# A graph-attention layer on one core: copies of the group loop moved to ScalarE, other superblock sizes at the end, the last quad divided by groups

## The chip, the cores and the metric

The kernel runs on one core of one Trainium2 chip. The metric is the device time of one execution in microseconds (us), less is better. Engines are called TensorE (PE in profiles), VectorE (DVE), ScalarE (ACT), GpSimd (POOL) and SyncE (SP).

## What is computed

A graph with 12,500 nodes of 128 features and 200,000 edges, sorted by destination. Each node's features are normalised and clipped at zero, multiplied by a weight matrix, and each edge gets four attention logits (one per head). Per destination node the logits go through a softmax over the incoming edges, and the source rows are summed with those weights.

```
h   = (max(layernorm(x), 0) @ W_node.T).reshape(N, 4, 32)
att = leaky(a . [h[src], h[dst], (edge_attr @ W_edge.T).reshape(E, 4, 32)])
m   = max(segment_max(att, dst), 0)
ex  = exp(att - m[dst])
denom = segment_sum(ex, dst) + (E - degree) * exp(-m)
out = x + segment_sum(ex / denom[dst] * h[src], dst)
```

## The kernel before

**Tiling.** Edges lie in 392 groups of 511 (four columns of 128 lanes, `J` = 4). Lane 0 of column 0 is kept for a row that carries the partial sum of a node from the group before. Four groups are a quad (98 of them, `QG` = 4), and a few quads a superblock. A group's destinations lie in a window of 96 nodes (`WIN`). A node's table row (`ROW` = 137 numbers) holds four heads of 32 values with a one behind each, a count of one (`R_CNT`) and four source logits (`R_SRC`).

**Stages.** A node stage writes the table. GpSimd meanwhile gathers raw node rows for quads 0 to 3, which `converted` (L236) later turns into table rows on the core: transposes, a copy, matmuls, copies by ScalarE (L262), then two memsets of ones by VectorE (L264, L266). From quad 4 on, `gather` (L127) fetches table rows: one indirect DMA per group and column (L136), 16 per quad, into a `ga` buffer of which there are 8. The buffer comes free when the sums of the quad eight places earlier are done.

**The group loop** has four kinds of steps per quad or superblock:

- `fetch` (L471): edge features `ea`, destinations `db`, side rows `pw`, node rows `xw`, issued by SyncE two quads ahead; `db` has two buffers.
- `logits` (L492) for each group: one comparison by VectorE (L499), six matmuls (L504, L507); then `add_sources` (L510) per quad, two VectorE instructions, of which L521 is the first to read the gathered rows.
- `softmax` (L532) per superblock: a chain of about twenty VectorE instructions on tiles of 511 columns, with transposes by TensorE and two exps by ScalarE (L589, L591).
- `sums` (L642) per quad: two small VectorE copies (L653 into `hot`, L654 from the PSUM tile `ex_ps` into `ga`); then for each group L660 (rows times weights), L663 (one-hot of the destinations), three matmuls (L668), and `complete` (L616), which works one group late: for the group before, L633 scales the carried row out of the PSUM tile `acc`, L637 copies its count, and the last matmul L639 follows; for the group before that, L624 copies `acc` to `pt`. One group after a quad's last copy, `divide` (L673) makes the output of all four groups with six VectorE instructions (L679 to L692) and SyncE writes four windows (L695). Windows of neighbouring groups overlap.

**Order.** The order on each engine is the order written here; nothing reorders it. `together` takes one step of each generator in turn. For superblock s the main loop (L769) runs `sums` of the last quad of s-1 beside the logits of the first quad of s+1 and the softmax of s; then `sums` of each quad of s but the last, each beside the logits of one more quad of s+1; logits left over follow alone. `add_sources` of a quad comes at the next logits or softmax, so L521 of a superblock's last quad stands at the start of its softmax. The end (L786 to L789) is `sums` of quad 97 and three calls of `complete`.

Superblocks are sized by `ends` (L427): two of 2 quads in front, then 22 of 4, then 2, 2, 1, 1.

Of the kernel before, what the change touches and what calls it, by code (L numbers as in the profile page):

```python
# [12 lines left out]
OP = mybir.AluOpType  # L13
AX = mybir.AxisListType

P = 128
H, HD = 4, 32
HW = HD + 1
D = H * HD
# [3 lines left out]
TINY = 1e-30  # L23


R_CNT, R_SRC, ROW = H * HW, H * HW + 1, H * HW + 5

J = 4
GE = J * P
NE = GE - 1  # L30
WIN = 96
QG = 4
# [3 lines left out]
NODE_T = 9  # L36
RAW = 4
SETS = max(NODE_T, QG * J)
PAD = 1 << 20


def blocks(total, step):
    return [(i, min(step, total - i)) for i in range(0, total, step)]
# [3 lines left out]
def kernel(  # L47
# [35 lines left out]
    nc = tc.nc  # L83
# [21 lines left out]
    ones = consts.tile([P, P], F32, name="ones")  # L105
# [7 lines left out]
    is_last = consts.tile([P, G, J], BF16, name="is_last")  # L113
# [5 lines left out]
    quads = blocks(G, QG)  # L119
    nq = len(quads)  # L120
# [26 lines left out]
    with tc.manual_schedule():  # L147
# [33 lines left out]
        def statistics(pool, rows, T):  # L181


            assert nc.vector.BN_STATS_DIM == 6
            stats = pool.tile([P, SETS, 6], F32, name="stats")
            for t in range(T):
# [3 lines left out]
            two = stats[:, :T, :].rearrange("p t (o k) -> p t o k", k=3)  # L190
            both = pool.tile([P, SETS, 2], F32, name="both")
            nc.vector.tensor_tensor(both[:, :T, :], two[:, :, 0, 1:3], two[:, :, 1, 1:3], op=OP.add)
# [43 lines left out]
        def converted(q, psum, turn_pool, copy):  # L236

            ga = GA[q]
            m = quads[q][1]
            made = []  # L240

            def turned_over(i):
                hT_ps = psum.tile([P, 512], F32, name="acc")
                hT_ps = hT_ps.rearrange("p (j e) -> p j e", j=J)
                for j in range(J):
                    nc.tensor.transpose(hT_ps[:, j, :], ga[:, i, j, 0:D], ident)
                hT = turn_pool.tile([P, J, P], F32, name="hT_e", bufs=2)
                copy(hT, hT_ps)
                made.append(hT)

            turned_over(0)
            for i in range(m):
                yield
                if i + 1 < m:
                    turned_over(i + 1)
                for k in range(J // 2):
                    row_ps = psum.tile([P, 512], F32, name="acc")
                    row_ps = row_ps.rearrange("p (j e) -> p j e", j=2)
                    for j in range(2):
                        nc.tensor.matmul(row_ps[:, j, :ROW], made[i][:, 2 * k + j, :],  # L260
                                         wcat, start=True, stop=True)
                    nc.scalar.copy(ga[:, i, 2 * k:2 * k + 2, :], row_ps[:, :, :ROW])  # L262
            rows = ga[:, :m].rearrange("p g j r -> p (g j) r")
            nc.vector.memset(  # L264
                rows[:, :, 0:H * HW].rearrange("p t (h w) -> p t h w", w=HW)[:, :, :, HD], 1.0)
            nc.vector.memset(rows[:, :, R_CNT:R_CNT + 1], 1.0)  # L266
            yield


# [16 lines left out]
        with tc.tile_pool(name="node", bufs=2) as node, tc.tile_pool(  # L286
# [48 lines left out]
            ends = [3, 6]  # L335
# [88 lines left out]
    per = SBG // QG  # L424


    ends = [2, 2], [2, 2, 1, 1]  # L427
    amid = max(nq - sum(ends[0]) - sum(ends[1]), 0)
    supers = []
    for m in ends[0] + [n for _, n in blocks(amid, per)] + ends[1]:  # L430
# [5 lines left out]
    with tc.tile_pool(name="work", bufs=2) as work, \  # L436
            tc.tile_pool(name="turned", bufs=1) as turned, \
            tc.tile_pool(name="ps", bufs=1, space=bass.MemoryType.PSUM) as ps:
        XW, LG, AT, U, DR = {}, {}, {}, {}, {}
# [4 lines left out]
        share_ps = const_ps[0:WIN, WIN + G:].rearrange("p (g h) -> p g h", h=H)  # L444
# [7 lines left out]
            g0 = quads[q0][0]  # L452
            return g0, quads[q0 + m - 1][0] + quads[q0 + m - 1][1] - g0

        def windows(q):
            g0, m = quads[q]
            return nc.values_load_multi_w_load_instructions(
                base[0:1, g0:g0 + m], engines=[mybir.EngineType.SP], min_val=0, max_val=N - 1,
                skip_runtime_bounds_check_because="a destination, which is a node")[1]
# [154 lines left out]
        state = {}  # L614

        def complete():  # L616

            division = state.pop("division", None)
            ready = full.pop() if full else None
            if begun:  # L620
                complete_group(ready[-1] if ready else state.get("before"), *begun.pop())
            if ready:
                q, i, pt, acc = ready
                nc.vector.tensor_copy(pt[:, i, :], acc)  # L624
                state["before"] = pt[:, i, :]
                if i == quads[q][1] - 1:
                    state["division"] = q, pt
            if division:
                divide(*division)

        def complete_group(before, q, i, ga, hot, pt, acc, fc):
            if before is not None:
                nc.vector.tensor_tensor(  # L633
                    ga[0:1, i, 0, 0:H * HW].rearrange("p (h w) -> p h w", w=HW),
                    before[WIN:WIN + 1, 0:H * HW].rearrange("p (h w) -> p h w", w=HW),
                    fc.unsqueeze(2).to_broadcast([1, H, HW]), op=OP.mult)
                nc.vector.tensor_copy(ga[0:1, i, 0, R_CNT:R_CNT + 1],  # L637
                                      before[WIN:WIN + 1, R_CNT:R_CNT + 1])
            nc.tensor.matmul(acc, hot[:, i, 0, :], ga[:, i, 0, :], start=False, stop=True)  # L639
            full.append((q, i, pt, acc))  # L640

        def sums(q):  # L642

            g0, m = quads[q]
            s = of_quad[q]
            s0, sm = groups(s)
            ga = GA.pop(q)
            heads = lambda t: t[:, :, 0:sm * H].rearrange("p j (h g) -> p j h g", h=H)
            ex, tops_at, facs = XS[s]
            fc = facs[WIN:WIN + 1, 0:sm * H].rearrange("p (h g) -> p h g", h=H)  # L650
            pt = work.tile([WIN + 1, QG, ROW], F32, name="pt", bufs=3)
            hot = work.tile([P, QG, J, WIN + 1], F32, name="hot")
            nc.vector.tensor_copy(hot[:, :m, :, WIN], is_last[:, g0:g0 + m, :])  # L653
            nc.vector.tensor_copy(  # L654
                ga[:, :m, :, R_SRC:R_SRC + H],
                heads(tops_at)[:, :, :, g0 - s0:g0 - s0 + m].rearrange("p j h g -> p g j h"))
            for i in range(m):
                g = g0 + i
                val = ga[:, i, :, 0:H * HW].rearrange("p j (h w) -> p j h w", w=HW)
                nc.vector.tensor_tensor(  # L660
                    val, val, heads(ex)[:, :, :, g - s0].unsqueeze(3).to_broadcast([P, J, H, HW]),
                    op=OP.mult)
                nc.vector.tensor_tensor(  # L663
                    hot[:, i, :, 0:WIN], lane_ps.unsqueeze(1).to_broadcast([P, J, WIN]),
                    slot[:, g, :].unsqueeze(2).to_broadcast([P, J, WIN]), op=OP.is_equal)
                acc = ps.tile([P, 512], F32, name="acc", bufs=3)[0:WIN + 1, 0:ROW]
                for j in range(1, J):
                    nc.tensor.matmul(acc, hot[:, i, j, :], ga[:, i, j, :], start=j == 1, stop=False)  # L668
                complete()
                begun.append((q, i, ga, hot, pt, acc, fc[:, :, g - s0]))  # L670
                yield

        def divide(q, pt):  # L673


            g0, m = quads[q]
            xw = XW.pop(q)
            others = work.tile([WIN, QG], F32, name="others")
            nc.vector.tensor_scalar(others[:, :m], pt[0:WIN, :m, R_CNT], -1.0, float(E),  # L679
                                    op0=OP.mult, op1=OP.add)  # L680
            den = work.tile([WIN, QG, H], F32, name="den")
            nc.vector.tensor_tensor(den[:, :m, :], pt[0:WIN, :m, R_SRC:R_SRC + H],  # L682
                                    others[:, :m].unsqueeze(2).to_broadcast([WIN, m, H]), op=OP.mult)
            val = pt[0:WIN, :m, 0:H * HW].rearrange("p g (h w) -> p g h w", w=HW)
            nc.vector.scalar_tensor_tensor(den[:, :m, :], val[:, :, :, HD], TINY, den[:, :m, :],  # L685
                                           op0=OP.max, op1=OP.add)
            nc.vector.reciprocal(share_ps[:, :m, :], den[:, :m, :])  # L687
            res = work.tile([WIN, QG, D], F32, name="res")
            nc.vector.tensor_tensor(  # L689
                res[:, :m, :].rearrange("p g (h d) -> p g h d", d=HD), val[:, :, :, 0:HD],  # L690
                share_ps[:, :m, :].unsqueeze(3).to_broadcast([WIN, m, H, HD]), op=OP.mult)
            nc.vector.tensor_tensor(res[:, :m, :], res[:, :m, :], xw[:, :m, 0:D], op=OP.add)  # L692
            at = windows(q)
            for i in range(m):
                nc.sync.dma_start(out[bass.ds(at[i], WIN), :], res[:, i, :])  # L695

        def all_logits(q):
# [291 lines left out]
```

## Time and profile before

| what | value |
|---|---|
| time, median of 3 runs | 2089.68 us (2087.87 to 2090.39) |
| time of the profiled execution | 2088.72 us |
| span of that execution | 2086.8 us |
| VectorE busy | 1563.0 us (75%), 4349 instructions |
| GpSimd busy | 1497.2 us (72%), 1574 instructions |
| TensorE matmuls busy | 1367.9 us (66%), 7275 instructions |
| ScalarE busy | 134.4 us (6%), 311 instructions |
| granted TensorE clock, mean | 0.537 |
| HBM traffic | 142 GB/s over the span |

The span runs from the first to the last instruction of the profiled execution; what lies around it is 1.9 us. The page gives for each engine its busy time, and for each group of equal instructions the line, the engine, output and inputs, the count, and after the bar the busy time in all, the mean time of one in ns, and the idle time ahead of them with what ended it. The timeline has one row per instruction: start, duration, engine, line, and in brackets the engine's idle time before it and what released it. "Issue" means that the profile shows no releaser.

### The profile page before, as it was taken

The page shows a single profiled execution, that of the slowest core. Times are in us where ns is not written, and L with a number is a line of the kernel's source. Part 1 is how long each engine was busy: PE and PEld are TensorE (multiplying, and loading weights), DVE is VectorE, ACT ScalarE, POOL GpSimd, SP SyncE. Part 2 cuts the span into 40 slices and gives each one's busy share as a digit, 9 for nine tenths or more (in the row PEclk, how much of TensorE's full clock was granted, in tenths as well). Part 3 has the DMA queues.
Part 4 walks back from the last instruction along what each step waited for, and adds up shares of the span by engine and source line. Part 5 has one row for each costly group of instructions (what it writes and reads, how often), then busy time and mean ns, then how long its engine had stood idle before and what let it go on. Part 6 is the DMA issues. An engine that isn't in the chain of part 4 may idle for free. (4 is left out here: it accounts for less than half of the span.)

```text
span 2086.8 us, 27038 instructions
## 1 busy us (share of the span) xinstructions
PE 1367.9 (66%) x7275; PEld 1239.8 (59%) x7275; DVE 1563.0 (75%) x4349; ACT 134.4 (6%) x311; POOL 1497.2 (72%) x1574
## 2 busy tenths in 40 slices
PE   5677688656657666666656667566576666666664
PEld 4566577656656556556556556565565565566553
DVE  7666798766877777777767768667677777778997
ACT  6651000000000000000000000000000000000000
POOL 7676577777777777777777777777777777777730
PEclk9765555555555555555555555555555555555655
DMA  7664667766566566656556565565656565565520
GB/s 255 191 160 113 157 154 168 161 143 153 140 149 151 136 147 143 145 142 145 149 133 150 139 143 144 138 147 134 152 139 146 138 153 145 139 144 143 123 63 15
DMA packets 214476, 298.95 MB, mean 143 GB/s; under 512 B 86121, under 2 KB 162153, under 8 KB 204914
## 3 DMA queue, kind: packets, MB, share of 16 engines
q1 hardware_dynamic: 162960, 185.77, 35.0%
q0 software_dynamic: 50112, 109.65, 23.6%
q10 hardware_dynamic: 1250, 1.78, 0.2%
q8 instruction: 60, 0.98, 0.2%
q14 instruction: 94, 0.77, 0.1%
HBM read 270.49 MB, written 26.52 MB: 142 GB/s over the span
## 5 line engine op out<-in xcount | busy, mean ns | idle before, releaser
L136 POOL DMA_INDIRECT ga<-table,srci x1502 | 1435.2, 956 | 490.6 <-issue 471.1
L668 PE MATMUL acc<-ga,hot 128*97 128x137 f32 x2352 | 644.4, 445 | 95.8 <-DVE hot L663 95.2
L668 PEld LDWEIGHTS acc<-ga,hot 128*97 128x97 f32 x2352 | 510.7, 275 | 122.6 <-DVE hot L663 111.1
L504 PEld LDWEIGHTS <-at 96*128 96x128 bf16 x1568 | 211.4, 164 | 526.6 <-DVE at L499 502.1
L504 PE MATMUL lg<-pw,at 96*128 96x12 bf16 x1568 | 169.2, 181 | 450.8 <-DVE at L499 433.8
L507 PE MATMUL lg<-wblk,ea 128*128 128x8 f32 x1568 | 408.4, 358 | 0.0
L507 PEld LDWEIGHTS lg<-wblk,ea 128*128 128x128 f32 x1568 | 381.0, 308 | 0.0
L521 DVE TENSOR_TENSOR U<-st,ga 128x64 f32<-128x64 f32 x98 | 26.2, 268 | 336.5 <-DMA ga<-table,srci 335.1
L499 DVE TENSOR_TENSOR at<-const_ps,db 96x512 bf16<-96x512 f32 x392 | 267.2, 683 | 12.0 <-DMA db<-in_dst_dram 8.0
L660 DVE TENSOR_TENSOR ga<-ga,ex_ps 128x528 f32<-128x528 f32 x392 | 269.9, 688 | 0.2
L639 PE MATMUL acc<-ga,hot 128*97 128x137 f32 x784 | 257.1, 431 | 0.5 <-DVE ga L637 0.5
L663 DVE TENSOR_TENSOR hot<-const_ps,slot 128x384 f32<-128x384 f32 x392 | 213.9, 546 | 0.0
L639 PEld LDWEIGHTS acc<-ga,hot 128*97 128x97 f32 x784 | 199.3, 283 | 0.7 <-DVE ga L637 0.7
L589 ACT ACTIVATE ex<-ex 64x512 f32<-64x512 f32 (+2 forms) x28 | 17.6, 629 | 1856.6 <-DVE ex L588 1856.6
L633 DVE TENSOR_TENSOR ga<-acc,facs 1x132 f32<-1x132 f32 x390 | 115.6, 296 | 16.6 <-PE acc L639 4.7
L624 DVE COPY pt<-acc 97x137 f32<-97x137 f32 x392 | 117.8, 301 | 12.7 <-PE acc L639 0.5
L136 POOL DMA_INDIRECT ga<-in_x_dram,srci x64 | 61.0, 953 | 20.9 <-issue 19.2
L692 DVE TENSOR_TENSOR res<-res,xw 96x512 f32<-96x512 f32 x98 | 67.5, 689 | 3.4
L689 DVE TENSOR_TENSOR res<-pt,const_ps 96x512 f32<-96x512 f32 x98 | 66.9, 683 | 3.4
L598 PE MATMUL ex_ps<-ident,ex 64*128 64x64 f32 (+2 forms) x112 | 18.6, 314 | 76.1 <-ACT ex L589 76.1
L598 PEld LDWEIGHTS ex_ps<-ident,ex 64*128 64x128 f32 (+2 forms) x112 | 13.8, 207 | 79.1 <-ACT ex L589 79.1
L637 DVE COPY ga<-acc 1x1 f32<-1x1 f32 x390 | 58.4, 150 | 0.0
(129 smaller groups left out, 984.6 us busy)
## 6 DMA issues: line engine op xcount, KB each, us to landing
db<-in_dst_dram SPq DMA_DIRECT2D x98, 768.0 KB
ea<-in_edge_t_dram SPq DMA_DIRECT2D x98, 512.0 KB
ga<-table,srci POOLq DMA_INDIRECT x1502
xw<-in_x_dram SPq DMA_DIRECT2D x392, 48.0 KB
out_dram<-res SPq DMA_DIRECT2D x392, 48.0 KB
pw<-side SPq DMA_DIRECT2D x392, 2.2 KB
table<-row SPq DMA_DIRECT2D x9, 616.5 KB
xt<-in_x_dram SPq DMA_DIRECT2D x9, 576.0 KB
```

Source lines behind the costliest of these rows:

```text
L136: nc.gpsimd.indirect_dma_start(out=ga[:, i, j, 0:width], out_offset=None, in_=rows, in_offset=bass.IndirectOffsetOnAxis(ap=srci[:, g0 + i, ...
L499: nc.vector.tensor_tensor(at[:, i, :], node_ps[0:WIN, g0 + i:g0 + i + 1].to_broadcast([WIN, GE]), db[:, i, :], op=OP.is_equal)
L504: nc.tensor.matmul(lg[:, i, j].rearrange("p k h -> p (k h)"), at[:, i, j * P:(j + 1) * P], sw, start=i + j == 0, stop=False, skip_group_ch ...
L507: nc.tensor.matmul(lg[:, i, 2 * w:2 * w + 2, 0, :], ea[:, i, w, :], wblk, start=False, stop=True, skip_group_check=True)
L624: nc.vector.tensor_copy(pt[:, i, :], acc)
L633: nc.vector.tensor_tensor(ga[0:1, i, 0, 0:H * HW].rearrange("p (h w) -> p h w", w=HW), before[WIN:WIN + 1, 0:H * HW].rearrange("p (h w) -> ...
L639: nc.tensor.matmul(acc, hot[:, i, 0, :], ga[:, i, 0, :], start=False, stop=True)
L660: nc.vector.tensor_tensor(val, val, heads(ex)[:, :, :, g - s0].unsqueeze(3).to_broadcast([P, J, H, HW]), op=OP.mult)
L663: nc.vector.tensor_tensor(hot[:, i, :, 0:WIN], lane_ps.unsqueeze(1).to_broadcast([P, J, WIN]), slot[:, g, :].unsqueeze(2).to_broadcast([P, ...
L668: nc.tensor.matmul(acc, hot[:, i, j, :], ga[:, i, j, :], start=j == 1, stop=False)
L689: nc.vector.tensor_tensor(res[:, :m, :].rearrange("p g (h d) -> p g h d", d=HD), val[:, :, :, 0:HD], share_ps[:, :m, :].unsqueeze(3).to_br ...
L692: nc.vector.tensor_tensor(res[:, :m, :], res[:, :m, :], xw[:, :m, 0:D], op=OP.add)
```

## The change

- In quads 0 to 13 and 92 to 97 (`HELPED`), L624, L637, L653 and L654 are issued to ScalarE in place of VectorE.
- In `converted`, the two memsets of ones become two ScalarE copies from the constant tile `ones`.
- The superblocks at the end have 3, 3, 2, 2, 2, 2 quads in place of 2, 2, 1, 1; the middle has 20 of 4 in place of 22, so that there are 28 in all as before.
- Quad 97 is divided and written group by group: `divide` takes a range of groups, and the registers with the window's place are loaded for that range.

```
+HELPED = 14, 6
...
-            nc.vector.memset(
-                rows[:, :, 0:H * HW].rearrange("p t (h w) -> p t h w", w=HW)[:, :, :, HD], 1.0)
-            nc.vector.memset(rows[:, :, R_CNT:R_CNT + 1], 1.0)
+            nc.scalar.copy(
+                rows[:, :, 0:H * HW].rearrange("p t (h w) -> p t h w", w=HW)[:, :, :, HD],
+                ones[:, 0:1].unsqueeze(2).to_broadcast([P, m * J, H]))
+            nc.scalar.copy(rows[:, :, R_CNT], ones[:, 0:m * J])
...
-    ends = [2, 2], [2, 2, 1, 1]
+    ends = [2, 2], [3, 3, 2, 2, 2, 2]
...
+        helped = lambda q: q < HELPED[0] or q >= nq - HELPED[1]
+        copier = lambda q: nc.scalar.copy if helped(q) else nc.vector.tensor_copy
...
-                nc.vector.tensor_copy(pt[:, i, :], acc)
+                copier(q)(pt[:, i, :], acc)
                 state["before"] = pt[:, i, :]
-                if i == quads[q][1] - 1:
-                    state["division"] = q, pt
+                if q == nq - 1:
+                    state["division"] = q, pt, i, i + 1
+                elif i == quads[q][1] - 1:
+                    state["division"] = q, pt, 0, i + 1
...
-                nc.vector.tensor_copy(ga[0:1, i, 0, R_CNT:R_CNT + 1],
-                                      before[WIN:WIN + 1, R_CNT:R_CNT + 1])
+                copier(q)(ga[0:1, i, 0, R_CNT:R_CNT + 1],
+                          before[WIN:WIN + 1, R_CNT:R_CNT + 1])
...
-            nc.vector.tensor_copy(hot[:, :m, :, WIN], is_last[:, g0:g0 + m, :])
-            nc.vector.tensor_copy(
+            copier(q)(hot[:, :m, :, WIN], is_last[:, g0:g0 + m, :])
+            copier(q)(
                 ga[:, :m, :, R_SRC:R_SRC + H],
                 heads(tops_at)[:, :, :, g0 - s0:g0 - s0 + m].rearrange("p j h g -> p g j h"))
...
-        def divide(q, pt):
+        def divide(q, pt, lo, hi):
+            n = hi - lo
+            xw = XW[q][:, lo:hi]
+            pt = pt[0:WIN, lo:hi]
...
-            at = windows(q)
-            for i in range(m):
+            at = windows(q, lo, hi)
+            for i in range(n):
                 nc.sync.dma_start(out[bass.ds(at[i], WIN), :], res[:, i, :])
```

More of the change, by code (lines that the diff above doesn't have):

```diff
@@ L453, in groups, with windows @@
             return g0, quads[q0 + m - 1][0] + quads[q0 + m - 1][1] - g0
-        def windows(q):
+        helped = lambda q: q < HELPED[0] or q >= nq - HELPED[1]
+        copier = lambda q: nc.scalar.copy if helped(q) else nc.vector.tensor_copy
+        def windows(q, lo=0, hi=QG):
             g0, m = quads[q]
+            g0, m = g0 + lo, min(hi, m) - lo
             return nc.values_load_multi_w_load_instructions(
@@ L671, in sums @@
                 yield
-        def divide(q, pt):
-            g0, m = quads[q]
-            xw = XW.pop(q)
+        def divide(q, pt, lo, hi):
+            n = hi - lo
+            xw = XW[q][:, lo:hi]
+            pt = pt[0:WIN, lo:hi]
             others = work.tile([WIN, QG], F32, name="others")
-            nc.vector.tensor_scalar(others[:, :m], pt[0:WIN, :m, R_CNT], -1.0, float(E),
+            nc.vector.tensor_scalar(others[:, :n], pt[:, :, R_CNT], -1.0, float(E),
                                     op0=OP.mult, op1=OP.add)
             den = work.tile([WIN, QG, H], F32, name="den")
[L682 to L685, printed above, removed]
+            nc.vector.tensor_tensor(den[:, :n, :], pt[:, :, R_SRC:R_SRC + H],
+                                    others[:, :n].unsqueeze(2).to_broadcast([WIN, n, H]), op=OP.mult)
+            val = pt[:, :, 0:H * HW].rearrange("p g (h w) -> p g h w", w=HW)
+            nc.vector.scalar_tensor_tensor(den[:, :n, :], val[:, :, :, HD], TINY, den[:, :n, :],
                                            op0=OP.max, op1=OP.add)
-            nc.vector.reciprocal(share_ps[:, :m, :], den[:, :m, :])
+            nc.vector.reciprocal(share_ps[:, :n, :], den[:, :n, :])
             res = work.tile([WIN, QG, D], F32, name="res")
             nc.vector.tensor_tensor(
-                res[:, :m, :].rearrange("p g (h d) -> p g h d", d=HD), val[:, :, :, 0:HD],
-                share_ps[:, :m, :].unsqueeze(3).to_broadcast([WIN, m, H, HD]), op=OP.mult)
-            nc.vector.tensor_tensor(res[:, :m, :], res[:, :m, :], xw[:, :m, 0:D], op=OP.add)
-            at = windows(q)
-            for i in range(m):
+                res[:, :n, :].rearrange("p g (h d) -> p g h d", d=HD), val[:, :, :, 0:HD],
+                share_ps[:, :n, :].unsqueeze(3).to_broadcast([WIN, n, H, HD]), op=OP.mult)
+            nc.vector.tensor_tensor(res[:, :n, :], res[:, :n, :], xw[:, :, 0:D], op=OP.add)
+            at = windows(q, lo, hi)
+            for i in range(n):
                 nc.sync.dma_start(out[bass.ds(at[i], WIN), :], res[:, i, :])
```

## The prediction

> **What bounds the kernel now.** I read the busy-by-slice rows, then the timeline of GpSimd, because L136 is the largest group of the page that runs without a break. The indirect gathers fill the `ga` buffers, 16 per quad, one every 1.25 us (0.94 busy, 0.30 between). Their timeline:
>
> ```profile
> 201.68 0.94 POOL L136 DMA_INDIRECT ga<-table,srci  x1 [8.41 <-issue]
> ...
> 257.40 0.94 POOL L136 DMA_INDIRECT ga<-table,srci  x1 [11.68 <-issue]
> ...
> 2008.30 0.94 POOL L136 DMA_INDIRECT ga<-table,srci  x1 [0.30 <-issue]
> ```
>
> The number in brackets is the idle time before the row. After the table is written (92.8 us) there are three gaps: 8.4 us before quad 9, 4.6 us at 225.95 before quad 10, and 11.7 us before quad 11, 24.7 us together. With 8 buffers, quad 9 needs the one of quad 1: the last L639 of quad 1 ends at 200.9, of quad 2 at 225.2, of quad 3 at 256.7, each 0.7 us before a gather resumes. From 257.4 to 2008.3 no gap follows. So the time has three parts: up to 257.4, where the sums of quads 1 to 3 hold the gathers; the gather stream, 1751 us, which the change leaves alone; and a tail after it. The windows view (PE, PEld, DVE, ACT, POOL busy; clock; DMA) shows whose tail that is:
>
> ```profile
> 350.00:1890.00 1540.00, 997.70 (x5248) 907.63 (x5247) 1131.92 (x3042) 21.83 (x38) 1167.62 (x1223) 0.51 0.61 145
> 1890.00:2010.00 120.00, 79.04 (x430) 70.48 (x430) 107.50 (x289) 3.45 (x6) 90.59 (x95) 0.59 0.50 123
> 2010.00:2079.00 69.00, 39.97 (x198) 33.93 (x198) 60.98 (x171) 2.29 (x4) 0.00 (x0) 0.60 0.05 13
> ```
>
> VectorE is 74% busy in the middle, 90% from 1890 and 88% after the last gather, when DMA is idle. ScalarE does almost nothing. The timeline of VectorE gives the places:
>
> ```profile
> 174.59 0.11 DVE L264 MEMSET ga<- 128x64 f32 x1 [10.98 <-ACT ga L262]
> ...
> 1892.87 0.27 DVE L521 TENSOR_TENSOR U<-st,ga 128x64 f32<-128x64 f32 x1 [6.01 <-DMA ga<-table,srci]
> ...
> 2045.20 0.27 DVE L521 TENSOR_TENSOR U<-st,ga 128x64 f32<-128x64 f32 x1
> ...
> 2067.23 0.30 DVE L633 TENSOR_TENSOR ga<-acc,facs 1x132 f32<-1x132 f32 x1 [0.31 <-PE acc L639]
> 2067.46 0.15 DVE L637 COPY ga<-acc 1x1 f32<-1x1 f32 x1
> 2067.64 0.30 DVE L624 COPY pt<-acc 97x137 f32<-97x137 f32 x1
> 2067.97 0.70 DVE L660 TENSOR_TENSOR ga<-ga,ex_ps 128x528 f32<-128x528 f32 x1
> ```
>
> L521 is the first use of a gathered quad. At quad 91 (1892.87) VectorE still waits for the gather; from quad 92 on it never does. Quad 97 is gathered at 2009.2 and used at 2045.20: VectorE is 33 us late at the end. The writes close the run:
>
> ```profile
> 2072.26 0.32 SPq L695 DMA_DIRECT2D out_dram<-res  x1
> ...
> 2083.08 0.32 SPq L695 DMA_DIRECT2D out_dram<-res  x1
> ```
>
> These are the first write of quad 96 and the last of quad 97. All eight are 1.53 us apart (1.71 between the quads, where registers are loaded): each waits for the one before. So the end is set by the division of quad 96, not by that of 97.
>
> **The Trainium skill.** "ScalarE: Activation LUTs", section What ACT_TABLE_LOAD costs, puts an ACTIVATE at 186 ns plus 0.833 ns per element, with neighbours overlapping by some 93 ns. The groups view agrees within 30 ns:
>
> ```profile
> L262 ACT COPY ga<-acc 128x274 f32<-128x274 f32 x32 | 12.0, 385 | 22.8 <-PE acc L260 22.6
> ...
> L248 ACT COPY hT_e<-acc 128x512 f32<-128x512 f32 x8 | 4.7, 584 | 19.6 <-PE acc L246 19.5
> ```
>
> "PSUM — Partial Sum Buffer", section Engine vs sequencer instructions, says the ScalarE and VectorE queues are strictly first in, first out; the 10.98 us above are that: everything queued behind a small memset waits. The same page, section on PSUM bank collisions, says that two engines on one bank must be kept apart, two reads included. No row here shows it (ScalarE and VectorE share no bank in these loops now), but the moved copies read `acc` and `ex_ps` beside VectorE's L633 and L660.
>
> **The change part by part.** Prices on VectorE, from the times at which the last L639 of a quad ends: sums of a quad alone 10.4 us (1931.1 to 1941.5), with the logits of another 13.1 (269.9 to 282.9), with a softmax too 23.6 (296.1 to 319.7), so a softmax is 10.5. A check: sums of four quads, two logits, one softmax make 57.5; L521 of quads 91 and 93 are 58.0 apart.
>
> *Ends of 12, 12, 8, 8, 8, 8 groups.* There are 28 superblocks before and after, so no softmax is added or dropped; only the order moves. Running the prices from quad 83 (used at 1732.5), with the gather ends of the trace plus 2.5 us to land:
>
> ```
> super   VectorE work from the use of its last quad       ends    last quad of the next usable
> 80-83   23.6 + 13.1 (waits to 1774) + 13.1 + 10.4        1798    86: 1793
> 84-86   23.6 + 13.1 + 13.1                               1848    89: 1853
> 87-89   23.6 + 13.1 + 10.4                               1900    91: 1893
> 90-91   23.6 + 13.1                                      1937    93: 1933
> 92-93   23.6 + 13.1                                      1974    95: 1974
> 94-95   23.6 + 13.1                                      2011    97: 2011.6
> ```
>
> VectorE is level with the gathers at the last one even with no help from ScalarE (helped, it has about 4 us in hand). So quad 97 is used at 2011.6 instead of 2045.2, 33.6 us earlier. What is given back: one more quad of sums then lies behind it (95, 96, 97 in place of 96, 97).
>
> *Copies to ScalarE.* L624 and L637 take 0.43 us of a VectorE group (0.74 from L633 to L660, 0.31 left), L653 and L654 0.2 per quad: 2 us of 13.1. On ScalarE, at 157 ns + 0.833 ns per element from the two rows above: 0.27 and 0.16 us per group, 1.7 us per quad, beside an engine idle there. But TensorE needs 2.94 us per group with logits at the granted half clock (198.79 to 201.74), 11.8 per quad, so only some 1.3 of the 2 us count there; sums alone need 1.94 (L668 1.48, L639 0.46), 7.8 per quad. The added waits: L639 now also waits for ScalarE's count copy, L660 for its copy out of `ex_ps` if the bank is guarded. Behind L660 VectorE queues L663 and so L668. Bounds: a gain of 0.5 us per superblock (VectorE no longer waits for L607) to a loss of 0.3; I take a loss of 0.15.
>
> *Tail after quad 97's use.* First the softmax beside sums of 95: 18.6 us before (2045.20 to 2063.84), less three groups of 0.43, so 17.3. Then sums of 96 and of 97 up to the division of 96. On VectorE: seven groups of 1.51 (L660 0.61, L663 0.57, L633 0.33) and two divisions of 2.3 (2069.92 to 2072.23), 15.2 in all; TensorE at 1.94 per group makes VectorE wait for L639 in most groups, some 2.3 us, so 17.5. Then the writes: four of 96 and four of 97, where the registers are now loaded per group, 4 x 1.53 + 0.2 + 3 x 1.71 = 11.4 (10.8 before). Last 3.7 us from the last write's issue to the end of the span, as before. Sum: 2011.6 + 17.3 + 17.5 + 11.4 + 3.7 = 2061.5, against 2086.8: **25.3 us earlier**.
>
> *Last quad group by group.* Each small division costs six VectorE instructions, about 1.4 us by the rows (0.2 for each of four, 0.3 for each of two), 5.6 in place of 2.3. They end before their writes, which queue behind those of 96, so this hides nothing and costs the 0.5 us above. If the writes did not queue it would give 2.8.
>
> *Ones by ScalarE.* Four VectorE stalls (3.1 at 107.4, 3.1 at 124.4, 2.5 at 149.2, 11.0 at 174.6) go. What is late next: at 107 ScalarE's own scaling (gain 0.4); at 124 nothing, VectorE is busy until 135 (3.0); at 149 the exps, and then the moved copies queue behind scaling on ScalarE (0, from 0.8); at 174.6 L521 needs L262's result anyway, and L660 waits for a copy that is queued behind it (-0.2, or +2 unguarded).
>
> *Front.* Saving at the end of quad 3's sums: 3.2 by 151 us; 0.8 in the sums of 0, where VectorE waits for L639; -0.2 at the stall; 2.8 by 210 (two groups alone, four beside TensorE, one superblock start); then SyncE's issue chain and the `db` load (210.6 to 231.9) carry it unchanged; 1.9 more by 256.7. Together **8.5 us**, of the 24.7 of gaps. Quads 9 and 10 then don't gate, and quad 12 keeps 7 us of slack. Bounds: 4 (TensorE limits every group) and 14 (no bank guard, full 2 us per quad).
>
> The span becomes 2061.5 - 8.5 = 2053.0. The profiled execution took 2088.72 with a span of 2086.8; the median is 2089.68, 1.0 above it. 2053.0 + 1.9 + 1.0 = **2055.9**.
>
> **Rivals.** (a) *The front gives nothing*: ScalarE's queue, full of scaling and conversions up to 174 us, holds the copies as long as VectorE did. For it: ScalarE is 12.3 of 17.5 us busy at 132 to 150. Against: the stall at 124. Then 2064.4. (b) *All gaps go*: 24.7 instead of 8.5, 2039.7; for it, quad 3's sums are only one chain; against it, SyncE's chain before 231.9. (c) *Superblocks of two fall behind*: 36.7 us against 40 of gathers is thin; 2 us more per quad in the sums of 86 to 97 are 24 us, less some 9 of slack (5 in the table at 1848, 4 by help): 15 later, 2071. (d) *Slower*: the hop L633, ScalarE's count copy, L639 becomes the loop from group to group. A group then takes the hop plus 1.0 us against 3.2 now in the front (16 groups before quad 11's gather) and 2.1 in the tail (12 groups). It eats the 33.8 us once the hop reaches 2.9 us; at 4 us the time is 2120. Against it: ScalarE rows of 0.16 to 0.39 us, with nothing long queued there after 175.
>
> **How the numbers follow.** Forecast 0.59; (a) 0.19; (b) 0.07; (c) 0.09; (d) 0.06, of which 0.04 with a hop long enough to be slower and 0.02 with one near 2.9 us, where the time is about the old one. Differences within 0.2% (2085.5 to 2093.9) are what a measurement can't tell from none. The forecast's own bounds are 2048 (14 in the front, no waits of 2.3 us for TensorE in the tail) and 2063 (4 in the front, small divisions that outlast their writes by 2 us). The range adds 1 us below for the spread of the runs, and above (a) and the nearer half of (c): 2047 to 2068. Faster 0.94, within 0.2% 0.02, slower 0.04.
>
> **What would show it.** Quad 97's L521 within 4 us of its gather and with a wait; gaps before quads 9 and 10 near nothing, before quad 11 near 16 at most with the last gather at about 2000; no L624 or L637 on VectorE in quads 0 to 13 and 92 to 97; the last eight writes back to back. Wrong if quad 97 is used more than 10 us after its gather, or the last gather starts later than 2004.

## The result, and the profile after

The kernel after takes 2057.23 us (median of 4 runs, 2054.11 to 2059.95), the kernel before beside it 2088.77 us (4 runs, 2086.60 to 2090.39). The ratio is 0.9849, with a 95% interval from 0.9830 to 0.9868: 31.5 us faster. The profiled execution took 2058.77 us with a span of 2057.0 us, at a mean granted clock of 0.538. Line numbers have shifted: the moved L624, L637, L653 and L654 are L631, L647, L663 and L664 in the kernel after, and L633, L639 and L660 are L643, L649 and L670.

The timeline of GpSimd, in the form shown of before (start, duration, and in brackets the idle time and what ended it), with the start of the stream, the two gaps left, and the last gather:

```profile
95.18 0.94 POOL L137 DMA_INDIRECT ga<-table,srci  x1 [11.87 <-DMA table<-row]
...
218.80 0.94 POOL L137 DMA_INDIRECT ga<-table,srci  x1 [3.24 <-PE acc L649]
...
249.56 0.94 POOL L137 DMA_INDIRECT ga<-table,srci  x1 [10.61 <-PE acc L649]
...
2001.79 0.94 POOL L137 DMA_INDIRECT ga<-table,srci  x1 [0.31 <-issue]
```

The gap before quad 9 is gone and the three gaps have shrunk from 24.7 to 13.9 us. Quad 11's gather starts 7.8 us earlier, the last gather ends at 2002.7 instead of 2009.2.

The windows view by stage (PE, PEld, DVE, ACT, POOL busy; clock; DMA), cut where this kernel's gathers end:

```profile
350.00:1890.00 1540.00, 997.44 (x5267) 907.25 (x5268) 1141.32 (x3049) 28.94 (x69) 1167.69 (x1222) 0.51 0.61 144
1890.00:2003.00 113.00, 81.31 (x446) 73.81 (x447) 102.40 (x260) 8.98 (x35) 85.87 (x89) 0.56 0.54 125
2003.00:2050.00 47.00, 27.16 (x126) 23.13 (x124) 35.41 (x95) 7.53 (x33) 0.00 (x0) 0.57 0.07 18
```

The middle is as it was. What is new is the length of the last row: 54.3 us pass from the end of the last gather to the end of the span, against 77.6 before. The timeline of VectorE shows why, and also what the copies brought with them:

```profile
170.31 0.70 DVE L670 TENSOR_TENSOR ga<-ga,ex_ps 128x528 f32<-128x528 f32 x1 [10.79 <-ACT ga L664]
...
2004.95 0.27 DVE L528 TENSOR_TENSOR U<-st,ga 128x64 f32<-128x64 f32 x1 [0.30 <-DVE st L526]
...
2022.80 0.70 DVE L670 TENSOR_TENSOR ga<-ga,ex_ps 128x528 f32<-128x528 f32 x1 [0.98 <-ACT ga L664]
...
2032.55 0.70 DVE L670 TENSOR_TENSOR ga<-ga,ex_ps 128x528 f32<-128x528 f32 x1 [0.74 <-ACT ga L664]
...
2042.57 0.28 DVE L700 TENSOR_TENSOR res<-pt,const_ps 96x128 f32<-96x128 f32 x1
...
2048.43 0.28 DVE L700 TENSOR_TENSOR res<-pt,const_ps 96x128 f32<-96x128 f32 x1 [3.68 <-DMA out_dram<-res]
```

L528 is the old L521, the first use of a gathered quad: quad 97 is used 2.2 us after the end of its gather (36.0 before). The 0.30 us that VectorE waits there are put down to its own instruction before, not to the gather, so it comes about when the gather lands, with nothing in hand. The stall of 11.0 us at 174.6, where VectorE waited to write ones, has become one of 10.8 us at 170.3, where it waits for ScalarE's copy out of `ex_ps`. The last row is a wait that nobody had looked for: `res` has two buffers, and the small division waits until an earlier write has landed.

The waits view of after (waiter, releaser, us in total, times, longest) puts sizes to this; the first row is idle time of ScalarE, which costs nothing:

```profile
ACT ga L647 <- DVE ga L643: 258.8, 77, 12.1
DVE ga L670 <- ACT ga L664: 20.5, 11, 10.8
POOL ga L137 <- PE acc L649: 14.2, 3, 10.6
DVE at L506 <- DMA db<-in_dst_dram: 8.3, 1, 8.3
DVE res L700 <- DMA out_dram<-res: 4.6, 4, 3.7
```

### The profile page after: what moved, and what is told of

Read it like the earlier page. It is cut to its first block, busy times and chain, and to the rows that moved or that the text cites. A ratio compares the mean times of both kernels' runs of the same rounds, so it can differ in the third digit from the quotient of the medians.

```text
span 2057.0 us, 27142 instructions
## 1 busy us (share of the span) xinstructions
PE 1363.9 (66%) x7275; PEld 1237.4 (60%) x7275; DVE 1532.7 (75%) x4160; ACT 173.8 (8%) x518; POOL 1498.8 (73%) x1574
## 3 DMA queue, kind: packets, MB, share of 16 engines
q10 hardware_dynamic: 1250, 1.78, 0.3%
## 5 line engine op out<-in xcount | busy, mean ns | idle before, releaser
L670 DVE TENSOR_TENSOR ga<-ga,ex_ps 128x528 f32<-128x528 f32 x392 | 270.1, 689 | 20.9 <-ACT ga L664 20.5
L528 DVE TENSOR_TENSOR U<-st,ga 128x64 f32<-128x64 f32 x98 | 26.3, 269 | 324.2 <-DMA ga<-table,srci 322.3
L649 PE MATMUL acc<-ga,hot 128*97 128x137 f32 x784 | 256.2, 430 | 0.6 <-ACT ga L647 0.6
L649 PEld LDWEIGHTS acc<-ga,hot 128*97 128x97 f32 x784 | 198.1, 281 | 0.9 <-ACT ga L647 0.9
L643 DVE TENSOR_TENSOR ga<-acc,facs 1x132 f32<-1x132 f32 x390 | 115.6, 296 | 22.2 <-PE acc L649 10.3
L631 DVE COPY pt<-acc 97x137 f32<-97x137 f32 x312 | 93.8, 301 | 9.9 <-ACT ga L647 0.2
L700 DVE TENSOR_TENSOR res<-pt,const_ps 96x512 f32<-96x512 f32 (+1 forms) x101 | 67.3, 667 | 8.5 <-DMA out_dram<-res 4.6
L703 DVE TENSOR_TENSOR res<-res,xw 96x512 f32<-96x512 f32 (+1 forms) x101 | 67.9, 673 | 3.5
L375 PE MATMUL row_ps<-wcat,hT 128*128 128x137 f32 x198 | 39.3, 348 | 20.8 <-DVE tgt L381 11.1
```

The costliest lines, as they stand in the source:

```text
L631: copier(q)(pt[:, i, :], acc)
L643: nc.vector.tensor_tensor(ga[0:1, i, 0, 0:H * HW].rearrange("p (h w) -> p h w", w=HW), before[WIN:WIN + 1, 0:H * HW].rearrange("p (h w) -> ...
L670: nc.vector.tensor_tensor(val, val, heads(ex)[:, :, :, g - s0].unsqueeze(3).to_broadcast([P, J, H, HW]), op=OP.mult)
L700: nc.vector.tensor_tensor(res[:, :n, :].rearrange("p g (h d) -> p g h d", d=HD), val[:, :, :, 0:HD], share_ps[:, :n, :].unsqueeze(3).to_br ...
L703: nc.vector.tensor_tensor(res[:, :n, :], res[:, :n, :], xw[:, :, 0:D], op=OP.add)
```

## The experiments

**Theory**: the sizes at the end let VectorE meet the last gather, and shorten the tail by themselves; the copies shorten VectorE's groups at the front, and so the gaps of the gathers; the two add up. **Rivals**: the sizes work only together with the copies; or the copies count for nothing, because something else (TensorE, a load) holds the gathers at the front.

### The parts taken apart, on the kernel as it is

Four edits, two of them tried on other chips again. New sizes alone (e1): the kernel before with

```
-    ends = [2, 2], [2, 2, 1, 1]
+    ends = [2, 2], [3, 3, 2, 2, 2, 2]
```

The old sizes in the kernel after (e2) are that edit the other way. The ones back on VectorE (e4) restores the two memsets. No help at the front (e5) is

```
-HELPED = 14, 6
+HELPED = 0, 6
```

e1, first run: 

> The kernel before with the new superblock sizes at its end and nothing else. Theory (the order of the work at the end makes the gain, VectorE keeps level with the gathers by itself): quad 97 is first used within 5 us of the end of its gather; the three gaps of the gathers in the front stay at 24.7 us; the end lies 18.6 + 18.8 + 10.9 + 3.7 us after that use, so about 2064 us of span and 2066 us of time. Rival (superblocks of two quads only keep up with ScalarE's help): quad 97 is used more than 10 us after its gather, 2075 us or more.

e1, again on two more chips: 

> The kernel before with nothing changed but the superblock sizes at the end, once more, to meet the gather stream as the bound. Theory (the end's gain is that of the sizes, and the front's that of the copies, so the two add up): the three gaps of the gathers before quads 9, 10 and 11 stay at 24.7 us together; quad 97 is first used within 5 us of the end of its gather; about 2066 us. Rival (the sizes gain only together with the copies on ScalarE, because VectorE alone falls behind in superblocks of two quads): quad 97 is used 10 us or more after its gather, 2075 us or more.

e2: 

> The changed kernel with the old superblock sizes at its end (2, 2, 1, 1). Theory: the front keeps its gain (gaps of about 14 us, 7 to 8 us less than before with the spread of the start), VectorE is again late, quad 97 is used some 25 us after its gather, and the help gives another 8 us or so in the last six quads: 2071 to 2075 us. Rival (the copies on ScalarE are the main gain, the sizes are a detail): 2063 us or less.

For e2 on a second chip 2071 to 2078 us were expected, with the same theory and rival.

e4: 

> The changed kernel with the two memsets of ones back on VectorE. Theory: the VectorE stalls at about 124 and 174 us return, and quad 3's sums end some 3 us later: the three gaps are 17 us in place of 14, the time 2060 us. Rival (ScalarE's own work bounds that part, so the stalls cost nothing): gaps and time as with the change, 2057 us.

e5: 

> The changed kernel with the four copies of quads 0 to 13 back on VectorE; ones and the end as changed. Theory: the copies give 4 to 5 us of the front: gaps of 18 to 19 us, 2061 to 2062 us. Rival (ScalarE's queue holds the copies back as long as VectorE took for them): gaps of 14 us, 2057 us.

On the three chips that these runs met, the kernel before itself takes 2856 to 2900 us, so each ratio is to the kernel before on the same chip and none can be set beside the 0.9849.

| edit | chip's kernel before | this kernel | ratio, 95% interval |
|---|---|---|---|
| e1 new sizes alone | 2863.55 | 2863.80 | 0.9989, 0.9968 to 1.0011 |
| e1 on a second chip | 2899.83 | 2889.88 | 0.9972, 0.9959 to 0.9984 |
| e1 on a third chip | 2855.62 | 2853.07 | 0.9988, 0.9972 to 1.0003 |
| e2 old sizes, copies, ones | 2863.55 | 2844.74 | 0.9932, 0.9906 to 0.9957 |
| e2 on the second chip | 2899.83 | 2891.79 | 0.9982, 0.9970 to 0.9995 |
| e4 after, ones by VectorE | 2863.55 | 2843.65 | 0.9925, 0.9893 to 0.9956 |
| e5 after, no help in front | 2863.55 | 2852.27 | 0.9953, 0.9933 to 0.9973 |

Why they say nothing on the theory is seen in the largest GpSimd group. It is from the page of e1 on the third chip; the sizes were all that differed from the kernel before, where 471 of the 491 us of idle time are "issue", nearly all of it the 0.30 us between two gathers:

```profile
L136 POOL DMA_INDIRECT ga<-table,srci x1502 | 1424.5, 948 | 1215.4 <-PE acc L639 569.3
```

Here the gathers wait for L639, the sums' last matmul, 78 times from 517 to 2706 us, 569 us in all. The waits view of the same run has at its head

```profile
DVE ga L633 <- remote: 835.7, 112, 12.2
PEld acc L639 <- DVE ga L637: 585.0, 85, 11.0
```

"Remote" is a wait whose end the trace has no releaser for; these last 7.5 us on average. L633 needs a result of TensorE whose matmuls the records, with their modelled ends, mostly show as over some us before; the mean granted clock in the records is 0.538 as elsewhere. So on these chips TensorE's results seem to be held up by something that the trace doesn't show, and the gather stream isn't the bound. It is so before the group loop too: the table gathers start at 161 to 162 us on these chips, against 93 to 95 on the others. With e1 on the second chip quad 97 is used at 2840.6, 77 us after its gather. That is the rival's sign by its letter, but VectorE is behind there for another reason, so it decides nothing. What can be read is only that where the stream doesn't bound, the new sizes are worth 0.1 to 0.3% by the medians, on two of the three chips not clear of the noise. The differences between e2, e4 and e5 aren't larger than that between e2's two chips.

### Two things seen in the profile after

The small copies at the start of a quad's sums back on VectorE (e6):

```
-            copier(q)(hot[:, :m, :, WIN], is_last[:, g0:g0 + m, :])
-            copier(q)(
+            nc.vector.tensor_copy(hot[:, :m, :, WIN], is_last[:, g0:g0 + m, :])
+            nc.vector.tensor_copy(
```

> The kernel after with the two small copies at the start of a quad's sums (into hot and out of ex_ps) back on VectorE; the copies of acc stay on ScalarE. Theory (on ScalarE these two stand behind the last count copy of the quad before, which waits for VectorE's scaling of the carried row, so VectorE stalls 0.7 to 1.0 us at every start of a quad in sums alone, and 10.8 us at 170 us behind the scaling of converted rows): the stalls of VectorE at the start of sums on ScalarE's copy go, the 10.8 us stall moves to the next instruction that needs the converted rows, the gaps of the gathers change by less than 1.5 us, and the time is level or up to 2 us better, 2055 to 2057 us. Rival (the moves of these two copies carry a real part of the front's gain): gaps 2 us or more longer, 2059 us or more.

A third buffer for the destinations (e7), `bufs=2` to `bufs=3` for `db`:

> The kernel after with three buffers in place of two for the destinations (db). Theory (the gap before quad 11 is no longer set by the speed of VectorE's groups but by the load of quad 8's destinations, which waits for its buffer to come free at 203.8 us, then queues behind other loads and lands at 225.5, so VectorE waits 8.3 us): the wait at 225 us shrinks to 4 us or less, the gap before quad 11 from 10.6 to about 5 us, the time is 2050 to 2053 us. Rival (the engines' work in quads 2 and 3 sets that gap, and the wait only moves to another place): gap before quad 11 above 9 us, 2056 to 2058 us.

Both met the second chip: 2880.87 us, ratio 0.9941 (0.9919 to 0.9963), and 2909.06 us, ratio 1.0030 (1.0016 to 1.0044). For the time both are inconclusive: neither was set beside the kernel after on that chip, and their gathers wait some 117 us before quads 8 to 11, where e7 was to change 5. That e7 is slower than even the kernel before stays unexplained. Of e6 one local reading holds, because the last quads' sums run there without such pauses. In its timeline of VectorE, the start of the sums of quad 97:

```profile
2843.00 0.30 DVE L643 TENSOR_TENSOR ga<-acc,facs 1x132 f32<-1x132 f32 x1
2843.33 0.18 DVE L663 CAST hot<-is_last 128x16 f32<-128x16 bf16 x1
2843.53 0.22 DVE L664 COPY ga<-ex_ps 128x64 f32<-128x64 f32 x1
2843.67 0.69 DVE L670 TENSOR_TENSOR ga<-ga,ex_ps 128x528 f32<-128x528 f32 x1
```

From L643 to L670 pass 0.67 us. In the kernel after it is 1.04 (2031.51 to 2032.55, the row with 0.74 shown above): L663 and L664 stand on ScalarE behind the count copy of the quad before, which can't start until L643 has ended. In e7, on the same chip as e6, it is 1.04 too. In quads of sums alone these two copies are 0.37 us better off on VectorE.

### The parts taken apart, with TensorE made light

To have the gather stream as the bound even where TensorE is slow, three kernels leave out part of the computation: the edge term of the logits, but for the last two columns of each quad, so that the `ea` buffers are still held as long. In all three (L504 to L508 of before):

```
                     nc.tensor.matmul(lg[:, i, j].rearrange("p k h -> p (k h)"),
                                      at[:, i, j * P:(j + 1) * P], sw,
-                                     start=i + j == 0, stop=False, skip_group_check=True)
-                nc.tensor.matmul(lg[:, i, 2 * w:2 * w + 2, 0, :], ea[:, i, w, :], wblk,
-                                 start=False, stop=True, skip_group_check=True)
+                                     start=i + j == 0, stop=j % 2 == 1, skip_group_check=True)
+                if i == m - 1 and w == 1:
+                    nc.tensor.matmul(lg[:, i, 2 * w:2 * w + 2, 0, :], ea[:, i, w, :], wblk,
+                                     start=False, stop=True, skip_group_check=True)
```

l1, the kernel before with it: 

> The kernel before with TensorE made lighter: the edge part of the logits (the matmuls of wblk by ea) is left out but for the last columns of a quad, so the logits lack that part. Nothing of VectorE, GpSimd or the DMAs changes. Purpose: TensorE's long pauses, which hold the gathers on the chips of the other runs, should go, so that the gather stream is the bound again. Theory: no gap of the gathers in the middle, VectorE waits for gathers in the middle and is 30 us or more late for quad 97, about 2080 to 2090 us. Rival (the pauses don't come from TensorE's load): gaps at every second quad as in the other runs, 2700 us or more.

l2, l1 with the new sizes: 

> The light kernel before (edge part of the logits left out in the same way) with nothing else changed but the superblock sizes at the end. Theory (the sizes alone bring the end's gain): quad 97 used within 5 us of its gather, gaps at the front as in the light kernel before, 18 to 25 us faster than it. Rival (only together with ScalarE's copies): quad 97 used 10 us or more after its gather, less than 15 us faster.

l3, the kernel after with it: 

> The kernel after with the edge part of the logits left out in the same way. Theory (copies and ones at the front add to the sizes at the end): the gaps of the gathers at the front are 8 to 14 us shorter than in the light kernel before, the last gather ends that much earlier, and the time is 5 to 12 us below that of the light kernel with the new sizes alone. Rival (the copies to ScalarE count for nothing, VectorE's own speed isn't what held the gathers): gaps and time within 3 us of that kernel.

They met a chip on which the kernel before takes 2087.07 us (8 runs), as in the result. So the long pauses were absent (whether light matmuls would end them stays untried), and the numbers compare directly. One thing more changed with the lighter work: the mean granted clock is 0.559 to 0.561 in these profiles, against 0.537 before. Ratios to the kernel before: l1 2078.58 us, 0.9960 (0.9946 to 0.9974); l2 2058.02 us, 0.9859 (0.9842 to 0.9875); l3 2043.71 us, 0.9791 (0.9775 to 0.9807). The timelines of the three, gaps of the gathers and first use of quad 97:

```profile
246.66 0.94 POOL L136 DMA_INDIRECT ga<-table,srci  x1 [12.93 <-issue]
...
2033.26 0.27 DVE L522 TENSOR_TENSOR U<-st,ga 128x64 f32<-128x64 f32 x1
```

```profile
248.68 0.94 POOL L136 DMA_INDIRECT ga<-table,srci  x1 [12.93 <-issue]
...
2002.42 0.27 DVE L522 TENSOR_TENSOR U<-st,ga 128x64 f32<-128x64 f32 x1 [0.45 <-DMA ga<-table,srci]
```

```profile
237.28 0.94 POOL L137 DMA_INDIRECT ga<-table,srci  x1 [2.71 <-PE lg L511]
...
1989.06 0.27 DVE L529 TENSOR_TENSOR U<-st,ga 128x64 f32<-128x64 f32 x1 [3.55 <-DMA ga<-table,srci]
```

The first row of each fence is the only gap left before quads 9 to 11; the second is quad 97's first use, which waits for its gather (the bracket) in l2 and l3 and not in l1 (L522 and L529 are the L521 and L528 of before and after). All five profiled executions by stage:

| us | table gathers start | gaps before quads 9 to 11 | last gather ends | quad 97 used | span ends |
|---|---|---|---|---|---|
| before | 92.84 | 24.7 | 2009.2 | 2045.2 | 2086.8 |
| after | 95.18 | 13.9 | 2002.7 | 2005.0 | 2057.0 |
| l1 light before | 93.30 | 12.9 | 1997.2 | 2033.3 | 2076.8 |
| l2 light, new sizes | 94.51 | 12.9 | 1999.9 | 2002.4 | 2056.0 |
| l3 light after | 94.06 | 2.7 | 1986.8 | 1989.1 | 2040.8 |

**The sizes alone** (l1 to l2) bring 20.6 us. The gap at the front is the same to the hundredth, and from the last gather to the end of the span it is 56.1 instead of 79.6 us, 23.4 less; 2.7 us of that were lost on the way to the last gather, in stages that are the same in both kernels. The rival (sizes only with copies) falls: without a copy on ScalarE quad 97 is used 2.5 us after its gather. The kernel as it is fits: its tail after the last gather is 23.3 us shorter than before.

**Copies, ones and the last quad** (l2 to l3) bring 14.3 us more, above the 5 to 12 that were expected (l1 too came out just under its 2080 to 2090): the gaps fall by 10.2 us, the last gather ends 13.1 us earlier (0.5 of it before the stream starts), and the tail after it is 54.0 instead of 56.1. To see what the copies do without the ones, the way from the first table gather to quad 11's is split at the first use of quad 3, where all the ones are written:

| us | to the first use of quad 3 | from there to quad 11's gather |
|---|---|---|
| before | 83.8 | 80.8 |
| after | 76.6 | 77.8 |
| l1 light before | 73.1 | 80.2 |
| l2 light, new sizes | 72.9 | 81.2 |
| l3 light after | 67.9 | 75.3 |

From l2 to l3 the second part falls by 5.9 us, so the rival (copies count for nothing) falls too. In the first part, 5.0 us less, ones and copies aren't told apart.

The two steps make 34.9 us in the light kernel. In the kernel as it is they make 31.5 together, and were not measured singly.

**TensorE's share**, not looked for: taking its work away with VectorE's unchanged (before to l1) closes 11.7 of the 24.7 us of gaps. So TensorE was part of what held the gathers. By the table nearly all of that lies ahead of quad 3's first use (83.8 to 73.1), where TensorE turns the raw rows of quads 0 to 3 into table rows beside the logits. It is 64.4 us busy there, in l1 46.6, with fewer matmuls and a mean granted clock of 0.73 instead of 0.62. After it light matmuls alone change little (80.8 to 80.2), but they decide how much of the copies' gain shows, 3.0 us with the full TensorE (before to after) and 5.9 with the light one. The windows view shows this for two quads (from the end of the sums of quad 4 to that of quad 6). Before:

```profile
269.90:296.10 26.20, 23.99 (x132) 22.70 (x129) 25.14 (x71) 0.00 (x0) 20.06 (x21) 0.50 0.71 147
```

After:

```profile
262.00:286.80 24.80, 23.96 (x129) 22.63 (x129) 21.76 (x50) 3.87 (x20) 18.71 (x21) 0.50 0.68 149
```

Light, new sizes (l2), then light after (l3):

```profile
260.90:286.80 25.90, 18.54 (x104) 16.41 (x102) 24.84 (x69) 0.00 (x0) 19.80 (x21) 0.57 0.66 150
```

```profile
248.50:271.70 23.20, 16.18 (x104) 14.81 (x102) 21.96 (x50) 3.86 (x20) 17.70 (x19) 0.65 0.66 156
```

The first number after the window is its length, then the busy time of PE, and as the third that of DVE. The copies take 3.4 us of two quads off VectorE. Of that, 1.4 us show in the kernel as it is, when TensorE is 23.96 of 24.8 us busy, which fits its taking over as the bound; with TensorE light 2.7 us show.

## Why the prediction was right

The forecast was 2055.9 us, measured 2057.2. Its mechanism holds at both ends. In the profiled execution the span is 4.0 us above the 2053.0 that was worked out, and the steps account for it: front 1.7 us better, stream 1.3 longer, tail 2.1 longer, and 2.3 us by which the table gathers started later. That start lies ahead of the copies, and l1 and l2, which don't differ up to there, are 1.2 us apart in it: so it is most likely a spread of executions, which the sum couldn't hold.

- **Ends of 12, 12, 8, 8, 8, 8.** Expected: quad 97 used 2.4 us after the end of its gather, instead of 36.0, with no help needed. Measured: 2.2 us, and 2.5 in l2 without help. The table of the working holds row by row: it puts the use of quads 86, 89, 91, 93, 95 and 97 at 1798, 1853, 1900, 1937, 1974 and 2011.6, without the front's gain; measured are 1791.6, 1849.4, 1897.2, 1933.7, 1970.2 and 2005.0, each 3 to 7 us earlier; the last gather is 6.5 earlier. The 4 us that the help was to leave in hand aren't there in the kernel after (a wait of 0.30 at quad 97), and are in l3 (3.55).
- **Copies to ScalarE.** That only part of VectorE's 2 us per quad would count beside TensorE was right, the part was too large: 1.3 expected, 0.7 measured (half of the 1.4 above). Light, where TensorE doesn't bind, it is 1.35. The Trainium skill asks for a guard of the PSUM bank ("PSUM — Partial Sum Buffer", section on PSUM bank collisions: two engines' reads of one bank must be ordered too). Such an order is in this trace: each ScalarE L647 on `acc` begins after VectorE's L643 on the same tile has ended, 0.03 us after it in nearly all, as in the rows below. Both also write the same row of `ga`, so the trace can't tell which of the two the order is for. The price at a superblock's start is near the worse bound of 0.3: from VectorE's last copy before it to L670 pass 0.98 us, where in l2 0.86 pass with both small copies still in between, so the 0.2 us counted as saved are gone and 0.12 more. Not in the working at all was the 0.37 us that each quad of sums alone loses, as e6 shows.
- **Ones.** The stalls at 107 and 124 are gone, in place of the one at 149 VectorE waits 1.78 us at 147 for a copy queued on ScalarE, and the fourth stays as a wait of 10.79 us for ScalarE's copy, as the working said. Its single gains were not measured apart.
- **Front.** Forecast 8.5 us, with bounds of 4 and 14. Quad 11's gather starts 7.8 us earlier, although the table was 2.3 us late; counted from the start of the table gathers it is 10.2. The excess lies ahead of 175 us: the first use of quad 3 comes 4.8 us earlier, or 7.2 from the table's start, where 3.8 was worked out. After that the working gave 4.7 us more and 3.0 came, which is the mis-sized part per quad. So two errors of opposite sign leave the sum only 1.7 us off, which is luck. What made the excess is open. TensorE's matmuls ahead of quad 3's first use, nearly the same number, took 59.8 us at a mean granted clock of 0.67, and 64.4 at 0.62 before; whether that came of the change or of chance no run tells. Quad 10 still waits, 3.2 us, where quads 9 and 10 were to be free. The `db` load at 231.9 is still there, at 225.6, with the same wait (8.3 us).
- **Tail.** Expected 49.9 us from quad 97's first use, measured 52.0. Its first two terms, 34.8, became 35.4. The term of the writes was mis-sized: 11.4 expected, 12.9 measured. It took the step from quad 96's last write to quad 97's first as 1.71 us, from the one execution of before; in after, l1, l2 and l3 it is 3.1 to 3.4. It isn't the change that makes it so: l1 and l2 divide as before, and in e4, e5 and e6, which divide as after, it is 1.6 (on the chips with the long pauses, whose other runs show 2.7 to 3.4). So the forecast that the eight writes go back to back fails at this one step, and the cause is open.
- **Last quad group by group.** It hides nothing, as forecast: the last issue comes 12.9 us after the first write of quad 96, 12.7 in l3, and 12.5 and 12.7 in l2 and l1, where quad 97 is divided whole. So it costs 0.4 us at most, where 0.5 was forecast. It wasn't tried by itself.

The timeline of after with the bank's guard in it, and the two issues with the long step between them:

```profile
2035.97 0.30 DVE L643 TENSOR_TENSOR ga<-acc,facs 1x132 f32<-1x132 f32 x1 [0.72 <-PE acc L649]
2036.30 0.70 DVE L670 TENSOR_TENSOR ga<-ga,ex_ps 128x528 f32<-128x528 f32 x1
2036.30 0.15 ACT L647 COPY ga<-acc 1x1 f32<-1x1 f32 x1 [1.77 <-DVE ga L643]
2036.48 0.27 ACT L631 COPY pt<-acc 97x137 f32<-97x137 f32 x1
...
2044.90 0.32 SPq L706 DMA_DIRECT2D out_dram<-res  x1
...
2048.34 0.32 SPq L706 DMA_DIRECT2D out_dram<-res  x1
```

L643 ends at 2036.27, and L647 follows 0.03 us later, while VectorE goes on with L670 at once: the order costs VectorE nothing here.

**The rivals.** (a) *The front gives nothing* is out: 10.8 us of gaps went, and l2 to l3 isolates it. (b) *All gaps go* is out in this kernel (13.9 us are left), but the light kernel comes to 2.7: the reason against it was wrong in part. The working named SyncE's chain and the `db` load as what stays; with the load's wait still in it (9.8 us in l3), the gap is nearly gone. From after to l3 quad 11's gather comes 11.2 us earlier, counted from the table's start, 8.7 of them ahead of quad 3's first use: what kept the gap open is in the main TensorE's work there. (c) *Superblocks of two fall behind* is out by quad 97's 2.2 us. (d) *The hop of the count copy becomes the loop* is out: it decides at 2.9 us, and L647 begins 0.03 us after L643 and lasts 0.15.

## What to carry to other kernels

When a queue of loads is the bound, read the two places where it isn't: how late its buffers come free at the start, and how far behind the consumer is at the last load; here the order of the work at the end was worth more than the instructions moved away. Of work moved off a busy engine only part counted here, where the next engine was nearly as busy in the same stage, so set both against the stage's length first. A small copy moved to an idle engine still stands in a queue there, as the 0.37 us of e6 show: see what is ahead of it, and what that waits for.

## What the runs showed of the hardware that wasn't expected

- On three of the four chips that the experiments met the kernel before took 2856 to 2900 us instead of 2087 us. Between 640 and 760 us of e1 on the third chip, TensorE shows 60.3 us of busy time where the kernel before, on a chip without this, shows 76.8, at mean granted clocks of 0.50 and 0.51, with engines waiting for matmuls that the records show as over. The granted clock doesn't show it, and the cause stays open.
- After the last write of quad 96 up to 3.4 us passed until the first of quad 97, where the four writes of quad 96 follow each other every 1.51 us. Over the 14 traces of this case that step is 1.6 to 3.4 us. With `res` in two buffers the small division waited 3.68 us for that landing; since the writes queue anyway, nothing was lost.
